# A GNN layer stack on one core: a small answer of SyncE to GpSimd behind every gather instead of behind every pair of gathers

## Chip, cores and metric

The kernel runs on one core of one Trainium2 chip. The metric is the device time of one execution in microseconds (us); the median of the runs is taken. One further execution is recorded by the hardware profiler, and all views of the profile come from that one.

## What is computed

Three layers of a relational graph network over 6250 nodes of 256 features and 100,000 edges, which come sorted by their target `dst`; then the input is added and a layer norm taken.

```python
ew = edge_attr @ edge_w + edge_b                       # 100000 x 256, from 32 attributes
for l in range(3):
    residual = x
    msg = relu(x[src] * ew)                            # x[src]: a gather of rows
    out = 0
    for i in range(3):                                 # three kinds of edge
        h = segment_sum(msg * rel_masks[i], dst) * inv_cnt[i]
        out = out + h @ weights[l, i]
    x = residual + relu(out + x @ roots[l] + biases[l])
return layernorm(x0 + x)
```

## The kernel before

**Tiles.** 128 edges make a tile, two tiles a pair (`u`, 391 of them in a layer), two pairs share one buffer `xs` of 128 x 2 x 2 x 256 floats, and there are eight such buffers (`ROWS = 8`, line 843). For each tile GpSimd (POOL in the profile) issues one indirect DMA that fetches 128 rows of 1 KB by the node numbers in `src_io`: 2346 gathers in all. In layer 0 they read the input, later `x_mid`, which the layer before has stored.

**What is done with a pair.** TensorE (PE) makes the edge weights in `ew_p` from the attributes `at` (lines 602 and 606); VectorE (DVE) multiplies them into `xs` (line 627), ScalarE (ACT) applies relu (629), VectorE makes one-hot columns of the targets (`oh`, line 635), TensorE reduces the messages into `h_p` (645), and VectorE adds that to a ring of sums `acc` (660). When a block of 128 nodes is complete, TensorE multiplies its sums by the weights (688), VectorE finishes the block (719, 722), and SyncE (SP) stores it to `x_mid` (724), or in the last layer to the output (741).

**Order.** The order of all instructions is written out by hand: one loop over steps `it` emits, for each step, the gathers of the pair nine steps ahead (`AHEAD = 9`) first, then SyncE's loads (`at`, line 560, once for eight pairs; in the last layer the input's blocks, line 748), then the work of the other engines. Each engine has its own instruction queue and goes through it in this order. The first six pairs of a layer are gathered early: for layer 0 before the main loop, into `x_root`, without the small exchange that is told of next; for the later layers at the end of the layer before (`gather_early`). Their missing rows are added by line 620 and 622. The first other gather of a layer waits until all blocks of `x_mid` have been stored, and the last block's store waits until the early gathers, which read the same tensor, have landed.

**The exchange with SyncE.** Behind the two gathers of a pair, `gather_pair` (line 899) lets GpSimd set one integer `echo` to nought (`memset`, line 905) and lets SyncE load it (line 906). Nobody uses the loaded value, and the compiled program has no load there any more: what is left on SyncE is a bare instruction that waits for the memset and counts up a semaphore (EVENT_SEMAPHORE of line 906). The next memset writes the same integer, so that GpSimd's sequencer must wait for that count first: an EVENT_SEMAPHORE of line 905 ahead of each memset. In GpSimd's instruction queue the order is: gather, gather, wait for SyncE's answer to the memset before, memset, gather, gather, wait, memset. A gather that uses an `xs` buffer again has an instruction of its own ahead of it that waits for the buffer's readers (EVENT_SEMAPHORE of line 901).

Of the kernel before, what the change touches and what calls it, by code (L numbers as in the profile page):

```python
# [442 lines left out]
def ordered_path(ctx, tc, x, attr_laid, A, weights, roots, biases, edge_w, edge_b, out, src, src_i, seg, place_i, consts, x_root,  # L443
# [126 lines left out]
    def layer(l, r_sb, b_sb, ats, early, pools):  # L570
# [12 lines left out]
        def gather(u):  # L583
            p = order.index(u)
            if p < FIRST:
                xs[u // 2] = early[u // 2]
            else:
                if first_of(p, 2):
                    xs[u // 2] = room(rows, D)
                gather_pair(nc, xs[u // 2], x_rows, src_i, u, echo)  # L590
# [18 lines left out]
        def gather_early(p):  # L609
            u = order[p]  # L610
            if first_of(p, 2):
                early_next[u // 2] = room(rows, D)
            gather_pair(nc, early_next[u // 2], x_mid[l], src_i, u, echo)
# [285 lines left out]
def gather_pair(nc, xs, x_rows, src_i, u, echo=None):  # L899
    for i in range(2):  # L900
        nc.gpsimd.indirect_dma_start(  # L901
            out=xs[:, u % 2, i, :], out_offset=None, in_=x_rows[:, :],
            in_offset=bass.IndirectOffsetOnAxis(ap=src_i[:, 2 * u + i:2 * u + i + 1], axis=0))
    if echo is not None:
        nc.gpsimd.memset(echo, 0)  # L905
        nc.values_load_multi_w_load_instructions(echo, engines=[mybir.EngineType.SP], min_val=0, max_val=0,  # L906
                                                 skip_runtime_bounds_check_because="it is nought")


@with_exitstack  # L910
def kernel(ctx, tc, x, src, dst, edge_attr, edge_type, weights, roots, biases, edge_w,
# [32 lines left out]
    with tc.tile_pool(name="look", bufs=1) as look, tc.tile_pool(name="look_p", bufs=2, space=PSUM) as look_p, \  # L944
# [17 lines left out]
        for u in schedule(N, E, 1)[0][:FIRST]:  # L962
            if u // 2 not in first_rows:
                j = 4 * len(first_rows)
                first_rows[u // 2] = x_root[:, j:j + 4, :].rearrange("p (k i) d -> p k i d", k=2)
            gather_pair(nc, first_rows[u // 2], x, src_i, u)
# [103 lines left out]
```

## Time and profile before

| | us |
|---|---|
| median of 3 runs | 2987.92 (2986.93 to 2989.48) |
| the profiled execution | 2990.14 |
| its span, from the first instruction to the last | 2988.3 |
| GpSimd busy | 2345.8 |
| TensorE: matmuls, weight loads | 2466.2, 2064.4 |
| VectorE busy | 2082.1 |
| ScalarE busy | 934.5 |

The granted TensorE clock is 0.897 on the mean. Busy time of GpSimd is that of the engine itself; what its sequencer does (waits for semaphores, hands instructions over) appears in the profile as POOLq, what SyncE's does as SPq. [...]

### The profile page before, as it was taken

The numbers are of one execution on the slowest core, as the hardware profiler recorded it, in microseconds if no ns is written. First come the engines' busy times: TensorE is split into PE (matmuls) and PEld (weight loads), VectorE is DVE, ScalarE is ACT, GpSimd is POOL, SyncE is SP. The second block draws the span as 40 slices with busy tenths as digits, with TensorE's granted clock in tenths as the row PEclk, the third lists the DMA queues.
The fourth block names the chain that finished last, engine by engine and source line by source line (L and its number), as shares of the span: only waits on it lengthen the run. The fifth ranks groups of instructions, "written<-read, shape, count | busy, mean of one in ns | idle before, by whom it ended". The sixth has DMA issues, their size and how long they took to land.

```text
span 2988.3 us, 58435 instructions
## 1 busy us (share of the span) xinstructions
PE 2466.2 (83%) x18875; PEld 2064.4 (69%) x18875; DVE 2082.1 (70%) x5868; ACT 934.5 (31%) x1155; POOL 2345.8 (78%) x3522
## 2 busy tenths in 40 slices
PE   5888888898988778888888888787888888888876
PEld 4777777777776666677676776565667677777765
DVE  7767777777776666666666666565767777787764
ACT  3333344444443222222222222222222222332221
POOL 7777787777777777777777777777777777777775
PEclk9899999999998888988999999788988989999987
DMA  5444444444444444444444444434444444444442
GB/s 169 137 144 135 145 126 127 128 128 130 132 130 118 121 130 120 125 125 123 127 128 130 127 130 133 122 120 143 133 134 139 134 131 137 137 128 129 132 124 87
DMA packets 173350, 388.09 MB, mean 130 GB/s; under 512 B 43418, under 2 KB 78636, under 8 KB 173036
## 3 DMA queue, kind: packets, MB, share of 16 engines
q0 software_dynamic: 112608, 307.65, 34.8%
q1 hardware_dynamic: 53136, 68.50, 7.4%
q10 hardware_dynamic: 7292, 8.11, 0.9%
q8 instruction: 154, 2.52, 0.3%
q14 instruction: 160, 1.31, 0.1%
HBM read 364.62 MB, written 19.46 MB: 129 GB/s over the span
## 4 chain that ended last, share of the span: by engine, by line
POOL 45%; PE 25%; issue 13%; DMA 9%; DVE 4%; ACT 1%; POOLq 1%; SPq 0%; DVEq 0%; ACTq 0%
POOL xs L901 43%; PE h_p L645 11%; DMA at<-in_attr_laid_dram 7%; PE ew_p L606 6%; PE o_p L688 5%; POOL echo L905 2%; PE r_p L673 2%; DVE xs L627 1%; DMA xs<-in_x_dram,src_io 1%; DMA xs<-x_mid,src_io 1%; ACT xs L629 1%; DVE oh L635 1%; PE ew_p L602 1%; DVE acc L660 1%; DVE x_root L719 0%
## 5 line engine op out<-in xcount | busy, mean ns | idle before, releaser
L901 POOL DMA_INDIRECT xs<-x_mid,src_io x1564 | 1490.2, 953 | 412.8 <-issue 236.7
L645 PE MATMUL h_p<-oh,xs 128*128 128x120 f32 x9336 | 1342.2, 296 | 151.6 <-DVE acc L660 87.8
L645 PEld LDWEIGHTS h_p<-oh,xs 128*128 128x128 f32 x9336 | 1252.8, 207 | 290.5 <-issue 123.2
L629 ACT ACTIVATE xs<-xs 128x1024 f32<-128x1024 f32 (+1 forms) x588 | 617.7, 1050 | 1769.3 <-DVE xs L627 1747.2
L627 DVE TENSOR_TENSOR xs<-ew_p,xs 128x512 f32<-128x512 f32 x1167 | 765.7, 684 | 555.1 <-PE ew_p L606 264.5
L901 POOL DMA_INDIRECT xs<-in_x_dram,src_io x770 | 734.2, 953 | 199.0 <-issue 117.7
L660 DVE TENSOR_TENSOR acc<-h_p,acc 128x240 f32 (+1 forms) x1173 | 518.6, 442 | 141.3 <-PE h_p L645 74.4
L606 PE MATMUL ew_p<-ew_sb,at 32*128 32x256 f32 x4692 | 401.1, 461 | 259.3 <-DMA at<-in_attr_laid_dram 255.9
L606 PEld LDWEIGHTS ew_p<-ew_sb,at 32*128 32x128 f32 x4692 | 263.9, 219 | 391.7 <-DMA at<-in_attr_laid_dram 354.9
L635 DVE TENSOR_SCALAR oh<-iota_w,seg_o 128x120 f32<-128x120 f32 x2346 | 517.7, 299 | 0.0
L688 PE MATMUL o_p<-w_sb,acc 128*128 128x256 f32 (+1 forms) x1716 | 456.8, 404 | 19.9 <-DVE acc L660 14.0
L688 PEld LDWEIGHTS o_p<-w_sb,acc 128*128 128x128 f32 (+1 forms) x1716 | 322.3, 200 | 87.8 <-issue 21.6
L719 DVE SCALAR_TENSOR_TENSOR x_root<-o_p,inv,x_root 128x256 f32<-128x256 f32 (+1 forms) x429 | 206.1, 480 | 56.4 <-PE o_p L688 49.1
L602 PE MATMUL ew_p<-bias,full_ones 3*128 3x512 bf16 x1173 | 166.9, 397 | 63.4 <-DVE xs L627 48.4
L673 PE MATMUL r_p<-r_sb,t_s 128*128 128x256 f32 x588 | 181.3, 437 | 5.9 <-ACT t_s L669 5.3
L639 ACT ACTIVATE oh_b<-oh 128x480 bf16<-128x480 f32 x196 | 117.8, 601 | 178.9 <-DVE oh L635 175.5
L705 ACT ACTIVATE acc<-zero_o 128x768 f32<-128x768 f32 (+1 forms) x150 | 140.6, 937 | 60.9 <-PE o_p L688 25.7
L673 PEld LDWEIGHTS r_p<-r_sb,t_s 128*128 128x128 f32 x588 | 117.9, 223 | 24.9 <-ACT t_s L669 9.4
L905 POOL MEMSET echo<- 1x1 int32 x1167 | 113.0, 97 | 1.2 <-SPq L906 0.9
L645 PE MATMUL h_p<-oh_b,full_ones 128*128 128x120 bf16 x782 | 108.2, 221 | 0.0
L676 DVE TENSOR_TENSOR x_root<-r_p,b_sb 128x256 f32<-128x256 f32 x147 | 61.8, 420 | 50.2 <-PE r_p L673 49.0
L645 PEld LDWEIGHTS <-full_ones 128*128 128x128 bf16 x782 | 82.7, 106 | 2.9
(93 smaller groups left out, 536.4 us busy)
## 6 DMA issues: line engine op xcount, KB each, us to landing
at<-in_attr_laid_dram SPq DMA_DIRECT2D x147, 256.0 KB
xs<-x_mid,src_io POOLq DMA_INDIRECT x1564
xs<-in_x_dram,src_io POOLq DMA_INDIRECT x770
x_mid<-x_all SPq DMA_DIRECT2D x96, 128.0 KB
x_all<-in_x_dram ACTq DMA_DIRECT2D x8, 768.0 KB
x<-in_x_dram SPq DMA_DIRECT2D x48, 128.0 KB
out_dram<-x_all SPq DMA_DIRECT2D x48, 128.0 KB
w_sb<-in_L_gnn_weights_dram SPq DMA_DIRECT2D x3, 768.0 KB
```

The source lines that it names most:

```text
L602: nc.tensor.matmul(banks[j].rearrange("p i d -> p (i d)"), full_ones[j * A:j * A + PARTS, :], bias[j * A:j * A + PARTS].rearrange("p i d - ...
L606: nc.tensor.matmul(banks[j][:, i, :], ats[OCT * o // GROUP][j * A:(j + 1) * A, o % (GROUP // OCT), i, :], ew_sb[j * A:(j + 1) * A, :], sta ...
L627: nc.vector.tensor_mul(xs[q][:, k], ew_ps[2 * q + k], xs[q][:, k])
L629: nc.scalar.activation(there, there, AF.Relu)
L635: nc.vector.tensor_scalar(ohs[q][:, t, :], iota_w, seg[:, 4 * q + t:4 * q + t + 1], None, op0=ALU.is_equal)
L645: nc.tensor.matmul(h_ps[u][:, d, :], xs[u // 2][:, u % 2, i, d * P:(d + 1) * P] if d < DC else full_ones, (ohs if d < DC else oh_bs)[u // ...
L660: nc.vector.tensor_tensor(there, h_ps[u][:, :CH].rearrange("p c (r w) -> p c r w", r=R), there, op=ALU.add)
L673: nc.tensor.matmul(rs[c][:, 1, :], t_ss[c][:, d, :], r_sb[:, d, :], start=(d == 0), stop=(d == DC - 1))
L688: nc.tensor.matmul(o_p[:n, j, :], acc[:, d, r, slot:slot + n], w_sb[:, r * DC + d, :], start=(d == 0), stop=(d == DC - 1))
L719: nc.vector.scalar_tensor_tensor(root, o_p[:n, j, :], inv[:n, c, r:r + 1], root, op0=ALU.mult, op1=ALU.add)
L901: nc.gpsimd.indirect_dma_start(out=xs[:, u % 2, i, :], out_offset=None, in_=x_rows[:, :], in_offset=bass.IndirectOffsetOnAxis(ap=src_i[:, ...
L905: nc.gpsimd.memset(echo, 0)
```

## The change

The memset and SyncE's answer move into the loop over the two gathers of a pair, so that they stand behind each gather.

```diff
     for i in range(2):
         nc.gpsimd.indirect_dma_start(
             out=xs[:, u % 2, i, :], out_offset=None, in_=x_rows[:, :],
             in_offset=bass.IndirectOffsetOnAxis(ap=src_i[:, 2 * u + i:2 * u + i + 1], axis=0))
-    if echo is not None:
-        nc.gpsimd.memset(echo, 0)
-        nc.values_load_multi_w_load_instructions(echo, engines=[mybir.EngineType.SP], min_val=0, max_val=0,
-                                                 skip_runtime_bounds_check_because="it is nought")
+        if echo is not None:
+            nc.gpsimd.memset(echo, 0)
+            nc.values_load_multi_w_load_instructions(echo, engines=[mybir.EngineType.SP], min_val=0, max_val=0,
+                                                     skip_runtime_bounds_check_because="it is nought")
```

In the compiled program that is 1167 more memsets on GpSimd with 1167 more waits for SyncE's answer ahead of them, and 1167 more answers on SyncE. The order of all other instructions is the same on every engine. GpSimd's queue becomes: gather, wait for SyncE's answer to the memset before, memset, gather, wait, memset.

## The prediction

> **What bounds the kernel.** I read the page first (busy times, the chain, the groups), then the stages, then GpSimd's own order of time.
>
> ```profile
> span 2988.3 us, 58435 instructions
> PE 2466.2 (83%) x18875; PEld 2064.4 (69%) x18875; DVE 2082.1 (70%) x5868; ACT 934.5 (31%) x1155; POOL 2345.8 (78%) x3522
> ...
> POOL 45%; PE 25%; issue 13%; DMA 9%; DVE 4%; ACT 1%; POOLq 1%; SPq 0%; DVEq 0%; ACTq 0%
> POOL xs L901 43%; PE h_p L645 11%; DMA at<-in_attr_laid_dram 7%; PE ew_p L606 6%; PE o_p L688 5%; POOL echo L905 2%; PE r_p L673 2%; DVE xs L627 1%; DMA xs<-in_x_dram,src_io 1%; DMA xs<-x_mid,src_io 1%; ACT xs L629 1%; DVE oh L635 1%; PE ew_p L602 1%; DVE acc L660 1%; DVE x_root L719 0%
> ...
> L901 POOL DMA_INDIRECT xs<-x_mid,src_io x1564 | 1490.2, 953 | 412.8 <-issue 236.7 <-SPq L906 141.1 <-PE h_p L645 8.2
> ...
> L905 POOL MEMSET echo<- 1x1 int32 x1167 | 113.0, 97 | 1.2 <-SPq L906 0.9
> ```
>
> TensorE is busiest by share, but the chain that ended last lies on GpSimd's gathers. GpSimd is 78% busy, so the question is whether its other 22% is free. The views of GpSimd's waits, of the gathers in one stage, and of its order of time say that it isn't:
>
> ```profile
> POOL xs L901 <- issue: 354.4, 1163, 0.6
> POOL xs L901 <- SPq L906: 206.8, 954, 0.2
> 1010.00:1975.00 965.00, 731.06 (x769) 0.89 0.42 126
> 62.70 0.95 POOL L901 DMA_INDIRECT xs<-in_x_dram,src_io  x1 [0.21 <-SPq L906]
> 63.95 0.95 POOL L901 DMA_INDIRECT xs<-in_x_dram,src_io  x1 [0.30 <-issue]
> 64.90 0.09 POOL L905 MEMSET echo<- 1x1 int32 x1
> 65.20 0.95 POOL L901 DMA_INDIRECT xs<-in_x_dram,src_io  x1 [0.22 <-SPq L906]
> ```
>
> In layer 1, 965 us hold 769 gathers, 965/769 = 1.255 us each, and a gather is busy 731.06/769 = 0.951. Gathers follow each other with a pause of 354.4/1163 = 0.305 that no event of the profile ends ("issue"). So GpSimd paces the kernel: a pair costs 2.51 us, whatever the rest does. An effect must change 1.25 us per gather, or GpSimd's few real stops. One nanosecond on each of 2346 gathers is 2.3 us; what a measurement of this kernel can tell from no change is about 0.2%, 6 us.
>
> **The memsets: 1167 more, put at 0.**
>
> ```profile
> L905 POOL MEMSET echo<- x1167: 88/88/255, 23.1 to 2965.3; 1x1 int32 x195
> L906 SPq EVENT_SEMAPHORE  x1168: 17/17/28, 26.6 to 2965.4; - x195
> SPq L906 <- POOL echo L905: 2744.2, 1166, 4.5
> ```
>
> A memset takes 0.088 at the median, and the pause behind it is 206.8/954 = 0.217. Together that is 0.305, the pause between two gathers without a memset. The order of time shows the same: 62.70 to 63.95 without, 63.95 to 65.20 with a memset, 1.25 each. The memset starts where the gather ends and lies inside a pause that is there anyway. Although the profile names SyncE's answer as what ended the 0.217, it can't be: gathers without it start at the same distance. So the 1167 memsets in the other pauses cost 0. If that cover failed they would cost 1167 x 0.097 (the group's mean, 113.0/1167) = 113 us, the upper bound; a gain is excluded, since no pause gets shorter with a memset in it.
>
> **The waits: the lead of GpSimd's sequencer.** Now the sequencer stops for SyncE's answer ahead of each memset, so behind a waiting instruction stands the memset and then the next gather. How early are gathers handed over today?
>
> ```profile
> L901 POOL DMA_INDIRECT xs<-in_x_dram,src_io x30: 942/946/1174, 20.7 to 58.9; - x30
> L901 POOL DMA_INDIRECT x_root<-in_x_dram,src_io x12: 942/948/1441, 5.1 to 19.4; - x12
> L901 POOLq EVENT_SEMAPHORE  x587: 17/43/43, 60.1 to 2958.0; - x196
> ```
>
> Up to 60.1 us, 30 + 12 = 42 gathers have started. The sequencer's first event of line 901, at 60.1, belongs to the first gather that uses an `xs` buffer again: after 12 gathers into `x_root` and 8 x 4 into the eight buffers, number 45, which starts at 62.70. So the sequencer works two gathers ahead, stopped by the answer. After the change it is one gather, 1.25 us, ahead. Is that enough? Two places show a gather handed over to an idle engine:
>
> ```profile
> 23.41 1.10 POOL L901 DMA_INDIRECT xs<-in_x_dram,src_io  x1 [0.15 <-issue]
> 24.82 1.10 POOL L901 DMA_INDIRECT xs<-in_x_dram,src_io  x1 [0.30 <-issue]
> 26.82 0.09 POOL L905 MEMSET echo<- 1x1 int32 x1 [0.91 <-SPq L906]
> 27.51 0.94 POOL L901 DMA_INDIRECT xs<-in_x_dram,src_io  x1 [0.59 <-issue]
> ...
> 1004.47 0.95 POOL L901 DMA_INDIRECT xs<-x_mid,src_io  x1 [0.30 <-issue]
> ...
> 1009.97 0.94 POOL L901 DMA_INDIRECT xs<-x_mid,src_io  x1 [4.47 <-DMA x_mid<-x_all]
> L901 POOLq EVENT_SEMAPHORE  x1: 43/43/43, 1009.2 to 1009.2; - x1
> L905 POOLq EVENT_SEMAPHORE  x1: 17/17/17, 1010.2 to 1010.2; - x1
> ```
>
> At 1009.2 the sequencer is released; the gather starts at 1009.97, 0.7 later, and at 1010.2 the sequencer has already handed over a second gather and stands at the next wait: 1.0 for two gathers, 0.5 each, the second while the first runs. At 26.82 the memset goes, and the gather behind it starts 0.69 later. After the change, the answer lets the sequencer go just after a memset; the gather that it then hands over is due 1.25 + 0.22 = 1.47 after that memset's end. It takes under 0.1 for the answer, 0.1 for the memset, 0.7 for the gather: 0.9. Some 0.5 us are left, so this too costs 0. The bounds: nothing, or, if no lead were left, 0.70 - 0.30 = 0.4 per gather. I take the first.
>
> **SyncE's queue.** 1167 x 17 ns = 20 us of answers, on an engine that waits 2744.2 us for these very memsets. Its DMA issues stay where they are, behind the answer to the pair's second memset, but the next answer is now due 1.25 us later instead of 2.5.
>
> ```profile
> 990.59 0.38 SPq L553 DMA_DIRECT2D r_sb<-in_L_gnn_roots_dram  x1
> 991.02 0.46 SPq L555 DMA_DIRECT2D b_sb<-in_L_gnn_biases_dram  x1
> 991.58 0.41 SPq L560 DMA_DIRECT2D at<-in_attr_laid_dram  x1
> at<-in_attr_laid_dram SPq DMA_DIRECT2D x147, 256.0 KB
> x_mid<-x_all SPq DMA_DIRECT2D x96, 128.0 KB
> x<-in_x_dram SPq DMA_DIRECT2D x48, 128.0 KB
> out_dram<-x_all SPq DMA_DIRECT2D x48, 128.0 KB
> ```
>
> The longest row of issues, at a layer's start, ends at 991.58 + 0.41 = 991.99, 1.4 after its begin: 0.2 late, under the 0.5 left. One or two issues of 0.4 fit in 1.25. So 0, at most 2 x 0.2.
>
> **The start: +2.5 us.** Here the added wait is seen. SyncE gives its first answer only at 26.6 (its row above), and today the second memset waits for it at 26.82, with gathers 15 and 16 (23.41 and 24.82) already gone. After the change the memset behind gather 14 waits, and gathers 15 and 16 stand behind it. The gather that starts at 27.51 will be the 15th instead of the 17th: two gathers at 1.25 later, 2.5 us. Nothing gives it back: the later stops, such as the 4.47 at 1009.97, begin when the last early gather has landed and shift with it.
>
> **The sum.** 0 + 0 + 0 + 2.5. Against the profiled execution's 2990.14 that is 2992.6; against the median, 2.2 lower, 2987.92 + 2.5 = **2990.4 us**, 0.08%: within what is told from no change.
>
> **The rivals.**
>
> *Late gathers (slower).* The lead of half a microsecond is worked out from idle starts; while a gather runs, handing over may take longer, and where SyncE issues a DMA the answer comes up to 0.3 to 0.4 later. Then the exchange becomes a wait on GpSimd's path at the 147 + 96 + 48 + 48 = 339 issues. It decides once handing over takes over 1.2 us. If each of these issues cost 0.05, that is 17 us, 3007; if each cost a third of a microsecond, 113 us. For it: nothing in the trace shows handing-over under load but for the second gather at 1010.2. Against it: that one was in time. Chance 0.25, at about 3007.
>
> *The memset isn't hidden (slower).* +113 us, 3103. It needs a pause of 0.305 that differs between first and second gathers of a pair; the x1163 and x954 rows speak against it. 0.07.
>
> *VectorE blocks the memset (slower).*
>
> ```profile
> L635 DVE TENSOR_SCALAR oh<-iota_w,seg_o x2346: 249/277/530, 33.4 to 2970.5; 128x120 f32<-128x120 f32 x196
> ```
>
> If a memset had to wait for the whole of a one-hot operation, it would last 0.088 + 0.277 = 0.365, 0.06 beyond the pause. 2346 x 0.277 / 2988 = 22% of the memsets would meet one: 1167 x 0.22 x 0.06 = 15 us, 3005. The longest memset of the trace is 0.255, inside the pause, among 1167, so 0.05. [...]
>
> *Fewer clashes (faster).* Gathers take 0.942 at best, 0.946 at the median, 0.953 on the mean (1490.2/1564 in the group shown at the start), so 7 ns x 2346 = 16 us go to clashes with other work. A new rhythm between GpSimd and VectorE may halve this: 8 us less, 2982. It may as well add them. 0.12.
>
> **How the numbers follow.** Forecast 0.51, late gathers 0.25, memset not hidden 0.07, blocked memset 0.05, fewer clashes 0.12. Slower by over 0.2% are the second to fourth, less 0.02 for late gathers that cost under 6 us: 0.35. Faster: 0.12. Within: 0.53. The range takes in the forecast's own, 2985 to 2996 (clashes of some us either way), half of the faster case at the low end, 2981, and late gathers up to 0.06 per issue, 2990 + 20 = 3010. Outside are the 113 us, the far end of late gathers and the rest of the faster case.
>
> **What would show it.** Right: gathers still 1.25 us apart, each with a memset of 0.088 and a pause of 0.217, x2334 memsets, the first answered memset at about 26.8 with the 15th gather behind it, the last gather about 2.5 us later. Late gathers would show as pauses over 0.22 behind memsets, ended by the answer of line 906, or as events of line 905 in GpSimd's sequencer that follow the answer by more than they do now. A hidden cost of the memset would show as a higher distance of gathers everywhere. Wrong is the whole argument if the distance of gathers in layer 1 leaves 1.255 by more than 3 ns.

## The result and the profile after

| us | before | after |
|---|---|---|
| median of 20 runs each | 2987.14 (2984.67 to 2994.27) | 2992.61 (2989.79 to 2997.78) |
| the profiled execution | 2990.14 | 2990.46 |
| its span | 2988.3 | 2988.7 |

The ratio is 1.0017, with a 95% interval of 1.0010 to 1.0023: 3.0 to 6.9 us longer, 5.5 by the medians. That is a small loss, below the 0.2% that the forecast took for what can be told from no change; but the forecast's 2.5 us lies under the interval, so the loss is about twice as large as forecast.

From the page of the changed kernel: span, busy times, the chain by engine and line, the groups of gathers and memsets. After them its view of GpSimd's waits (us in total, times, longest).

```profile
span 2988.7 us, 61936 instructions
PE 2457.0 (82%) x18875; PEld 2063.2 (69%) x18875; DVE 2080.9 (70%) x5868; ACT 934.2 (31%) x1155; POOL 2454.8 (82%) x4689
...
POOL 55%; PE 19%; issue 11%; DMA 7%; DVE 4%; POOLq 1%; ACT 1%; SPq 1%; DVEq 0%; ACTq 0%
...
L901 POOL DMA_INDIRECT xs<-x_mid,src_io x1564 | 1491.0, 953 | 338.7 <-SPq L906 309.0
...
L905 POOL MEMSET echo<- 1x1 int32 x2334 | 227.8, 98 | 4.3 <-SPq L906 3.8
```
```profile
POOL xs L901 <- SPq L906: 459.1, 2123, 0.6
...
POOL echo L905 <- SPq L906: 3.8, 1, 3.8
```

GpSimd's busy time has grown by 109 us (2454.8 - 2345.8), and the span by 0.4. The pause behind a memset is 459.1/2123 = 0.216 us, as before, and the 354.4 us of pauses put down to "issue" are now memset plus this pause. A reader who goes by the list of waits alone would say that SyncE's answer has come to hold GpSimd for 252 us more; the distance of the gathers says that it doesn't. The same 965 us of layer 1 as in the prediction, begun 2.4 us later, where this layer's first answered gather now starts (view by windows: us, GpSimd's busy time in gathers and their count, TensorE's clock, DMA share, GB/s):

```profile
1012.40:1977.40 965.00, 731.09 (x768) 0.89 0.42 125
```

965/768 = 1.2565 us for each gather, with 769 before: one gather fewer, the smallest step of such a count. The median distance of two gathers is 1.251 in both traces. The start, in GpSimd's order of time in the changed kernel:

```profile
22.11 0.95 POOL L901 DMA_INDIRECT xs<-in_x_dram,src_io  x1 [0.22 <-issue]
26.87 0.09 POOL L905 MEMSET echo<- 1x1 int32 x1 [3.82 <-SPq L906]
27.55 0.94 POOL L901 DMA_INDIRECT xs<-in_x_dram,src_io  x1 [0.59 <-SPq L906]
28.50 0.09 POOL L905 MEMSET echo<- 1x1 int32 x1
28.80 0.94 POOL L901 DMA_INDIRECT xs<-in_x_dram,src_io  x1 [0.22 <-SPq L906]
29.73 0.09 POOL L905 MEMSET echo<- 1x1 int32 x1
30.05 0.95 POOL L901 DMA_INDIRECT xs<-in_x_dram,src_io  x1 [0.23 <-SPq L906]
```

The gather at 27.55 is the 15th, so the 17th starts at 30.05, where it was 27.51 before: 2.5 us. The end, in the order of time of VectorE and GpSimd, first before, then after:

```profile
2964.37 0.94 POOL L901 DMA_INDIRECT xs<-x_mid,src_io  x1 [0.30 <-issue]
2969.34 0.69 DVE L627 TENSOR_TENSOR xs<-ew_p,xs 128x512 f32<-128x512 f32 x1 [3.48 <-DMA xs<-x_mid,src_io]
```
```profile
2968.47 0.95 POOL L901 DMA_INDIRECT xs<-x_mid,src_io  x1
2971.87 0.69 DVE L627 TENSOR_TENSOR xs<-ew_p,xs 128x512 f32<-128x512 f32 x1 [1.65 <-DMA xs<-x_mid,src_io]
```

The last gather starts 4.10 us later, but what follows it was shorter in this execution: 2988.7 - 2969.41 = 19.3 us from the last gather's end to the span's, and 23.0 before. The last rows landed earlier after it, and TensorE's clock was higher there (0.77 and 0.65):

```profile
2965.31:2988.30 22.99, 11.26 (x44) 9.49 (x43) 6.60 (x19) 2.40 (x4) 0.09 (x2) 0.65 0.06 17
```
```profile
2969.41:2988.70 19.29, 8.03 (x46) 7.02 (x45) 6.69 (x19) 2.40 (x4) 0.09 (x2) 0.77 0.07 21
```

In the profiled executions of these two kernels and of the experiments on chips like theirs this tail is between 18.4 and 23.8 us, with no order by kernel. So two spans must not be compared to the microsecond. The start of the last gather is free of the tail, but it still holds the lengths of all gathers, and in the experiments below with memsets of one integer, or with none, on chips like these two kernels' these add up to 0.25 to 1.94 us more than before. Its parts have to be told apart.

Where its 4.10 us come from I worked out from the starts and ends of all 2346 gathers in both traces. The first gather starts 0.14 later. The stop at the start is 2.90 longer (4.19 beyond the usual pause of 0.305, and 1.29 before). The two stops between layers are 0.15 shorter, the gathers themselves 0.39 shorter, the rest 0.07 shorter. What is left is new: 30 pauses of over 0.305 + 0.01 us, 1.66 us together beyond 0.305, where before had none. One of the two largest lies between 2324.99 and 2325.53 in the changed kernel:

```profile
2324.04 0.95 POOL L901 DMA_INDIRECT xs<-x_mid,src_io  x1 [0.22 <-SPq L906]
2324.99 0.09 POOL L905 MEMSET echo<- 1x1 int32 x1
2325.53 0.94 POOL L901 DMA_INDIRECT xs<-x_mid,src_io  x1 [0.46 <-SPq L906]
```

All 30 come behind a gather whose number leaves 7 when divided by 21 (112, 196, 238, 280, 364 and so on, the last 2338). There are 112 such places; 30 of them show a pause, of 0.02 to 0.24 us. Most of the 30 have something else in common: in 24 the gather that comes late uses an `xs` buffer again, so that the instruction of line 901 that waits for the buffer stands ahead of it in GpSimd's queue. Of the 111 places behind a memset 29 have that instruction, and 24 of these show a pause; of the other 82 only 6 do.

### The profile page after: what moved, and what is told of

Same layout as the page of the kernel before. It is cut to its first block, busy times and chain, and to the rows that moved or that the text cites. A ratio compares the mean times of both kernels' runs of the same rounds, so it can differ in the third digit from the quotient of the medians.

```text
span 2988.7 us, 61936 instructions
## 1 busy us (share of the span) xinstructions
PE 2457.0 (82%) x18875; PEld 2063.2 (69%) x18875; DVE 2080.9 (70%) x5868; ACT 934.2 (31%) x1155; POOL 2454.8 (82%) x4689
## 3 DMA queue, kind: packets, MB, share of 16 engines
q0 software_dynamic: 112608, 307.65, 34.9%
## 4 chain that ended last, share of the span: by engine, by line
POOL 55%; PE 19%; issue 11%; DMA 7%; DVE 4%; POOLq 1%; ACT 1%; SPq 1%; DVEq 0%; ACTq 0%
POOL xs L901 49%; PE h_p L645 8%; POOL echo L905 6%; DMA at<-in_attr_laid_dram 5%; PE o_p L688 4%; PE ew_p L606 4%; PE r_p L673 2%; DMA xs<-in_x_dram,src_io 2%; DVE xs L627 1%; SPq L906 1%; POOLq L905 1%; DMA xs<-x_mid,src_io 1%; ACT xs L629 1%; DVE oh L635 1%; DVE x_root L719 1%
## 5 line engine op out<-in xcount | busy, mean ns | idle before, releaser
L606 PE MATMUL ew_p<-ew_sb,at 32*128 32x256 f32 x4692 | 395.0, 455 | 249.8 <-DMA at<-in_attr_laid_dram 246.3
L905 POOL MEMSET echo<- 1x1 int32 x2334 | 227.8, 98 | 4.3 <-SPq L906 3.8
```

What stands on the lines that cost most here:

```text
L606: nc.tensor.matmul(banks[j][:, i, :], ats[OCT * o // GROUP][j * A:(j + 1) * A, o % (GROUP // OCT), i, :], ew_sb[j * A:(j + 1) * A, :], sta ...
```

## The experiments

All are the changed kernel but for the edit shown. The three groups ran on three chips, each group beside the kernel before on its own chip.

### The start and the lead: first group

My theory was that the start costs 2.5 us and that a lead of two gathers removes the small pauses. Before took 2987.03 us on this chip (33 runs).

*The start as before, the rest as after.*

```diff
-                gather_pair(nc, xs[u // 2], x_rows, src_i, u, echo)
+                gather_pair(nc, xs[u // 2], x_rows, src_i, u, echo, l > 0 or p >= FIRST + 2)    # each
...
-        if echo is not None:
+        if echo is not None and (i == 1 or each):
```

> The changed kernel, but the first two pairs of layer 0 that have an answer get one for each pair, as before; every other gather has its own. Theory (start plus pauses): the gather behind the first late answer is the 17th again instead of the 15th, so the last gather ends 2.5 us earlier than in the changed kernel; the some 30 pauses of 0.02 to 0.25 us (together 1.7 us) stay. Time 2.5 us under the changed kernel, about 1.7 to 2.5 above the kernel before. Rival (the added memsets disturb the rhythm of GpSimd and VectorE everywhere): the time stays where the changed kernel is, about 5 above before.

Measured: 2988.59 us, ratio 1.0009 [1.0000, 1.0018]. Its trace has the start of before again (the 17th gather at 27.70), and 33 small pauses, 2.28 us together. So the small pauses don't come from the start. The time alone would not tell: its interval reaches from 0 to 5.4 us above before.

*The kernel before, with a memset and an answer behind the first gather of the first answered pair too.* Here only that one pair is answered for each gather:

```diff
-                gather_pair(nc, xs[u // 2], x_rows, src_i, u, echo)
+                gather_pair(nc, xs[u // 2], x_rows, src_i, u, echo, l == 0 and p == FIRST)    # each; False for the early gathers
...
-        if echo is not None:
+        if echo is not None and (i == 1 or each):
```

> The kernel before, but the first pair of layer 0 that has an answer gets one behind each of its two gathers. Theory: it has the changed kernel's start alone, the 15th gather at 27.5 us, the last gather 2.5 us later than before and no pauses of 0.02 to 0.25 us, so 2.5 us above before. Rival: nothing, within 1 us of before.

Measured: 2990.22, ratio 1.0011 [1.0002, 1.0020], 3.3 us (0.6 to 6.0). By the middle of that, one memset and one answer make more than half of the 5.5. GpSimd's order of time in this kernel:

```profile
21.86 0.96 POOL L901 DMA_INDIRECT xs<-in_x_dram,src_io  x1 [0.23 <-issue]
26.75 0.09 POOL L905 MEMSET echo<- 1x1 int32 x1 [3.92 <-SPq L906]
27.43 0.94 POOL L901 DMA_INDIRECT xs<-in_x_dram,src_io  x1 [0.59 <-issue]
```

The 15th gather stands behind the late answer as in the changed kernel, and there is not one small pause. Its stop at the start is 3.01 longer than before. Its last gather starts 4.66 later all the same, because a stop between layers is longer and its gathers together last 1.18 more, which shows how little one execution's last gather says without its parts.

*Two integers in turn*, so that a memset waits for the answer to the memset before the last, and the sequencer's lead is two gathers again:

```diff
-    echo = big.tile([1, 1], I32, name="echo")
+    echo = [big.tile([1, 1], I32, name=f"echo{i}") for i in range(2)]
...
-            nc.gpsimd.memset(echo, 0)
+            nc.gpsimd.memset(echo[i], 0)
```

> The changed kernel, but the two gathers of a pair use an integer of their own each, so that a memset waits for the answer to the memset two before, and the sequencer can be two gathers ahead again, with as many instructions as in the changed kernel. Theory: the small pauses (33 over 0.315 us in the changed kernel, none before but three long ones) vanish; at the start the 16th gather, not the 15th, stands behind the late answer, so 1.25 us are lost instead of 2.5. Time 1.25 above before, some 3 under the changed kernel. Rival (pauses come from the larger number of instructions itself, or of memsets): the pauses stay, only 1.25 us are won.

Measured: 2988.57, ratio 1.0005 [0.9996, 1.0014]. No small pause is left, with the same 2334 memsets and answers. The 16th gather, not the 15th, comes first behind the late answer. So the pauses come from the lead, not from memsets or answers as such. The times of these three kernels overlap in their intervals; it is the traces that separate them.

*No memset and no answer at all.*

```diff
-        if echo is not None:
-            nc.gpsimd.memset(echo, 0)
...
```

> No memset and no answer at all. Theory (memsets and answers lie in a pause that is there anyway, and only the stop at the start costs): gathers still 1.25 us apart; the stop of 1.3 us at the start goes, time 1.3 us under before, 2986. Rival (the answers hold the sequencer back from something harmful): slower than before by over 6 us, with longer gathers or new pauses.

Measured: 2986.44, ratio 0.9999 [0.9990, 1.0008]. Without a single memset the gathers keep their distance. From this kernel's order of time:

```profile
704.23 0.95 POOL L901 DMA_INDIRECT xs<-in_x_dram,src_io  x1 [0.30 <-issue]
705.49 0.95 POOL L901 DMA_INDIRECT xs<-in_x_dram,src_io  x1 [0.30 <-issue]
706.74 0.95 POOL L901 DMA_INDIRECT xs<-in_x_dram,src_io  x1 [0.30 <-issue]
```

### What the pause covers, and where the 21 comes from: second group

This group fell to a chip on which the kernel before takes 4435.66 us (11 runs) and in whose records TensorE's clock is 0.75 to 0.84. GpSimd doesn't pace most kernels there (its memsets wait 1303.6 us for answers in the kernel with one more memset and 959.1 in the one with the memset of 128x128), so the times say nothing about the changed kernel on the first chip, and I read the traces where gathers follow each other undisturbed.

*One more memset, of an integer that nobody waits for.* My first idea of the 21 was that something recurs with the number of instructions; then one more instruction for each gather would make the grid shorter. The 18 gathers that I put for it were an estimate from a count of instructions for each gather that no run shows.

```diff
-    echo = big.tile([1, 1], I32, name="echo")
+    echo = [big.tile([1, 1], I32, name=n) for n in ("echo", "spare")]
...
+            nc.gpsimd.memset(echo[1], 0)
```

> The changed kernel with one more memset, of another integer that nobody waits for, behind each answered memset. In the changed kernel the small pauses stand 21 gathers, or multiples of 21, apart. [...] The second memset still fits in the pause of 0.305 (2 x 0.088), so the time is that of the changed kernel within 3 us. Rival (the pauses come from SyncE's loads, from blocks of nodes or another rhythm of the program): they stay 21 apart. Rival on the cover (each memset costs): 2334 x 0.09 = 210 us more.

Measured: 4637.91, ratio 1.0456 [1.0431, 1.0481]. The order of time in this kernel:

```profile
207.16 0.09 POOL L905 MEMSET echo<- 1x1 int32 x1
207.19 0.09 POOL L906 MEMSET spare<- 1x1 int32 x1
207.46 0.94 POOL L901 DMA_INDIRECT xs<-in_x_dram,src_io  x1 [0.19 <-issue]
208.40 0.09 POOL L905 MEMSET echo<- 1x1 int32 x1
208.43 0.09 POOL L906 MEMSET spare<- 1x1 int32 x1
208.71 0.95 POOL L901 DMA_INDIRECT xs<-in_x_dram,src_io  x1 [0.19 <-issue]
```

Gathers are 1.25 apart with two memsets as with one. The two overlap: the second starts 0.03 behind the first, so that together they take 0.12. Of the kernel's 43 pauses between 12 and 290 ns over the usual one, 28 stand on the grid of 21. They did not move to 18: the idea of the instructions fell.

*The memset without an answer*, on this chip:

```diff
             nc.gpsimd.memset(echo, 0)
-            nc.values_load_multi_w_load_instructions(echo, ...)
```

> The changed kernel's memset behind every gather, but no answer of SyncE and so no wait. Theory: nothing stops at the start and the lead isn't limited, so 1.3 us under before (the stop of 1.3 us at the start goes), no small pauses, gathers 1.25 us apart. Rival (the memsets themselves cost, by clashes or in the pause): above before, at the changed kernel's 5 us or more.

Measured: 3766.16, ratio 0.849 [0.8468, 0.8512]. I had expected next to nothing; on this chip the answers cost 15%. More on that at the end.

*A memset of 128x128 and one of 128x512 in place of one integer.*

```diff
-    echo = big.tile([1, 1], I32, name="echo")
+    echo = big.tile([128, 128], I32, name="echo")      # in the second kernel [128, 512]
...
-            nc.values_load_multi_w_load_instructions(echo, ...)
+            nc.values_load_multi_w_load_instructions(echo[0:1, 0:1], ...)
```

> The changed kernel with an integer tile of 128 x 128 set to nought instead of 1 x 1; the answer still loads one integer. The trace has one memset of 128 x 128, 0.204 us. Theory (a memset is free as long as it leaves some 0.06 us of the pause of 0.305, so up to 0.245): cadence still 1.25 us; time at most 15 us above the changed kernel, from memsets that clash and from an answer that comes 0.12 later. Rival (a memset is never free, its cost at 1 x 1 is only too small to see): 2334 x (0.204 - 0.088) = 271 us above the changed kernel.

> The same with 128 x 512, which by the sizes of the memsets in the trace takes some 0.45 to 0.7 us (m). Theory: beyond 0.245 each gather pays the rest, 2334 x (m - 0.245): 480 to 1060 us above the changed kernel, and the pause between a memset and the next gather falls to about 0.06 us. Rival (the memset runs beside the next gather, there is no limit): no change of the time.

Measured: 4394.42, ratio 0.9911 [0.9880, 0.9941], and 3949.97, ratio 0.8901 [0.8874, 0.8928]; neither time can be held against an expectation made for the first chip. From the order of time of the second:

```profile
207.04 0.95 POOL L901 DMA_INDIRECT xs<-in_x_dram,src_io  x1 [0.16 <-SPq L906]
207.99 0.54 POOL L905 MEMSET echo<- 128x512 int32 x1
208.69 0.95 POOL L901 DMA_INDIRECT xs<-in_x_dram,src_io  x1 [0.17 <-SPq L906]
```

The pause behind a long memset is 0.16 to 0.17, not the 0.06 that I had put as its floor. So a memset of this kind is free only up to 0.305 - 0.165 = 0.14 us, and my "free up to 0.245" fell for it. In the undisturbed stretches of the 128x128 kernel gathers are 1.34 apart, 0.09 more. With 128x512 the median distance is 1.657, 0.41 more than 1.251, where 0.54 - 0.14 is 0.40 and my theory had 0.30.

The 0.165 is no floor for memsets of one integer. In the changed kernel some of them last longer than 0.14, and the gather behind them still comes in time. The longest, in GpSimd's order of time:

```profile
2848.26 0.96 POOL L901 DMA_INDIRECT xs<-x_mid,src_io  x1 [0.23 <-SPq L906]
2849.21 0.26 POOL L905 MEMSET echo<- 1x1 int32 x1
2849.52 1.11 POOL L901 DMA_INDIRECT xs<-x_mid,src_io  x1
```

It has 0.05 behind it, and the pause between the two gathers is 0.305 as ever. So how much room the pause has depends on the memset; why a large one needs 0.165 behind it and a small one that takes long does not, no run shows.

### The scratch, the answer, the length: third group

The kernel is built with `dynamic_dma_scratch_size=4096`, by its name a scratch for dynamic DMAs; the profile lists the queue of the gathers' 307.65 MB as software_dynamic. My second idea was a guess: that GpSimd goes through this scratch as a ring, and that the grid of 21 is the turn of that ring. No trace shows such a ring. Before took 2987.00 us on this chip (19 runs).

*Half the scratch, and twice of it.*

```diff
-    nc = _bacc.Bacc(..., dynamic_dma_scratch_size=4096)
+    nc = _bacc.Bacc(..., dynamic_dma_scratch_size=2048)     # in the second kernel 8192
```

> The changed kernel with dynamic_dma_scratch_size=2048 in place of 4096, nothing else. Theory of the ring (the small pauses of the changed kernel, which stand at every 21st gather, come where GpSimd's ring of DMA descriptors turns over, and a lead of one gather doesn't cover it): half the ring turns over after about half the gathers, so the pauses stand on a grid of 10 gathers, and there are about twice as many (60 for 30, 3 us for 1.7); the time is 1 to 3 us above the changed kernel. Rival (the 21 comes from the tables or the buffers of the kernel, not from the ring): the grid stays 21, with some 30 pauses, and the time is that of the changed kernel within 2 us. If TensorE's clock on this chip is so low that GpSimd doesn't pace the kernel, the grid alone is read.

> The changed kernel with dynamic_dma_scratch_size=8192 in place of 4096, nothing else. Theory of the ring: a grid of 42 gathers and about half the pauses (15, under 1 us); the time is 0 to 1 us under the changed kernel. Rival (tables or buffers): the grid stays 21, with some 30 pauses and 1.7 us.

Measured: 2990.75, ratio 1.0013 [1.0004, 1.0023] with 2048, and 3020.60, ratio 1.0108 [1.0091, 1.0125] with 8192. The rival (a grid of 21 in any case) fell, and so did the numbers of my theory: I had expected more pauses with half the scratch and fewer with twice of it. With 2048 there is none (none over 0.011). With 8192 there are 47, at every 49th gather without exception, of 0.59 to 0.72 us, together 29.7; 3020.60 - 2990.75 = 29.9. One of them, in GpSimd's order of time with 8192, and then the sequencer's two events of line 905 on either side of it (duration, then first and last start):

```profile
578.07 0.94 POOL L901 DMA_INDIRECT xs<-in_x_dram,src_io  x1 [0.22 <-SPq L906]
579.00 0.09 POOL L905 MEMSET echo<- 1x1 int32 x1
580.02 0.94 POOL L901 DMA_INDIRECT xs<-in_x_dram,src_io  x1 [0.93 <-ACT oh_b L639]
```
```profile
L905 POOLq EVENT_SEMAPHORE  x1: 17/17/17, 577.9 to 577.9; - x1
...
L905 POOLq EVENT_SEMAPHORE  x1: 17/17/17, 579.8 to 579.8; - x1
```

The memset at 579.00 ends at 579.09, and SyncE's answer follows 0.04 later; the sequencer comes to it only at 579.8. Something ahead of it in GpSimd's queue held it from 577.9 to 579.8, 1.9 us, where the distance of such events is otherwise 1.25. ScalarE, whom the profile names as what ended the wait of 0.93, has nothing to do with it: in other such places it names SyncE or TensorE. At all 47 places the two events are 1.79 to 1.91 us apart (once 2.11), with the answer there 0.04 behind the memset. So at every 49th gather the handing over of a gather takes about 1.8 to 1.9 us, more than the lead of one gather covers. Where the gather handed over uses its buffer again (13 of the 47 places), the pause is longer, 0.69 on the mean for 0.61 at the others: line 901's instruction costs some 0.08.

The three sizes go together if the longer handing over grows with the scratch: 0.6 us beyond the lead with 8192, just at its edge with 4096 (30 of 112 places show it, by a mean of 0.055), inside it with 2048. That 4096 is at the edge fits the 24 of 30 pauses at which line 901's instruction is added; that there is a longer handing over with 2048 at all is not seen. The changed kernel with 4096 was not run on this chip, but the last kernel below has 4096: in 11 places its gather comes later behind the memset than the usual 0.165, and all 11 are on the grid of 21 (112, 196, 280 and so on). So the chip is not what took the grid away. That the scratch sets the grid and the length is shown by the edit of that one number; what the sequencer does at that place is not in the trace and stays open. With a lead of two gathers the place stays hidden with 4096 (two integers in turn, and before). The kernel before with 8192 was not run.

*The memset without an answer, on a chip like the first.*

> Each gather is followed by a float set to zero, as in the changed kernel, but SyncE answers none and GpSimd waits for none: 2334 memsets without an answer. All theories that hold the memset free: gathers 1.25 us apart as in both kernels, no small pauses, no stop at the start; where GpSimd paces the kernel, 1 to 2 us under the kernel before and 5 to 7 us under the changed one. If the memset cost what lies beyond a free pause, say 0.02 us for each, it would be 40 us above the kernel before.

Measured: 2985.90, ratio 0.9994 [0.9985, 1.0004]. Its 2334 memsets cost nothing that can be measured; the count by windows (us, gathers' busy time and count, clock, DMA share, GB/s) is that of before, 749 gathers in 940 us, 1.255 each:

```profile
1030.00:1970.00 940.00, 712.08 (x749) 0.92 0.43 126
```

*The memset of 128x128, on a chip like the first.*

> The changed kernel with a memset of 128x128 floats in place of one float. By the trace of this kernel on the other chip (0.226 us for the memset, 0.165 to 0.17 behind it, gathers 1.34 apart): 0.09 us for each of 2334 gathers, 210 us above the changed kernel, so about 3200 us, where GpSimd paces the kernel. By my older bound (a memset is free up to 0.245 us): no more than 5 us above the changed kernel.

Measured: 3197.85, ratio 1.0730 [1.0683, 1.0776]; about 207 above the changed kernel with 2048, which ran beside it, for 210 expected. Its groups by line (the memset's busy time and mean) and its order of time:

```profile
L905 POOL MEMSET echo<- 128x128 int32 x2334 | 528.7, 227 | 4.9 <-SPq L906 3.8
```
```profile
1500.17 0.95 POOL L901 DMA_INDIRECT xs<-x_mid,src_io  x1 [0.17 <-SPq L906]
1501.12 0.22 POOL L905 MEMSET echo<- 128x128 int32 x1
1501.50 0.95 POOL L901 DMA_INDIRECT xs<-x_mid,src_io  x1 [0.17 <-SPq L906]
```

0.22 + 0.165 is 0.08 beyond the pause, for each of 2334 gathers; over all gathers the pauses beyond 0.305 come to 196 us, and the gathers themselves are 8 us longer than with 2048. Each nanosecond that every memset adds to GpSimd's path counts 2334 times here, 1167 times for the memsets that the change adds: 5 ns for each would have been 6 us.

## Why the forecast held, step by step

**GpSimd paces the kernel: right.** 0.08 us on every gather (the 128x128 memset) made the kernel 7% slower; 0.63 at every 49th, 1%.

**The memsets at 0: right, by the reason given.** The pause stayed at 0.305 with no, one and two memsets. The prediction left open how much room there was: for the large memsets it is 0.14 us, and of the memsets of one integer, 0.088 at the median, even the longest, 0.263, cost nothing.

**VectorE blocks the memset: memsets are longer beside its one-hot operations, at no price.** 308 of the changed kernel's 2334 memsets last over 0.11 us, and all 308 run beside a TENSOR_SCALAR of VectorE, 298 of them beside the one-hot operations of line 635; none that runs beside VectorE's other operations alone, or beside none, is that long. 250 others run beside a TENSOR_SCALAR and last no longer than 0.11; what makes the difference no run shows. But the longest is 0.263, not the 0.365 that the rival needed, and it still lies inside the pause, as shown above:

```profile
L905 POOL MEMSET echo<- x2334: 88/88/263, 21.8 to 2969.4; 1x1 int32 x195
```

**The sequencer's lead at 0: mis-sized, by 1.7 us.** The step read: handing a gather over takes 0.7, the lead is one gather, some 0.5 us are left. That holds for the ordinary gather. But the 0.5 was read from two ordinary places, and handing over isn't the same for all: on a grid of 21 gathers it takes so long that little or nothing is left, and 30 times the gather comes late, 1.66 us in all, 24 of these times where the sequencer has the buffer's waiting instruction to go through as well. The rival "late gathers" had the right mechanism (a lead that no longer covers handing over) in the wrong place: not at SyncE's 339 DMA issues, which show no pause of their own, but on a grid that the DMA scratch sets, and at a tenth of its price. With a scratch of 8192 the same step costs 30 us, and the changed kernel takes 3020.60, outside the range of 2981 to 3010. That the term is small with 4096 is luck: nothing in the prediction looked at it.

**SyncE's queue at 0: right on chips like the first**, by the same grid: no small pause of the changed kernel stands off it.

**The start, +2.5: right.** 2.54 at the 17th gather, 3.3 [0.6, 6.0] in time for that edit alone. The stop itself is 2.90 longer; some of that comes back before the 17th gather, as gathers 14 to 16, of 1.10 to 1.17 each in the kernel before, now take 0.94 to 0.95.

**The sum.** 2.5 was forecast, under the measured 3.0 to 6.9. The two causes shown, the stop at the start with 2.90 and the small pauses with 1.66, make 4.6, and 4.1 is what the starts of the last gather show in one execution each; both lie inside that interval. Of the rest to the 5.5 of the medians, about 1 us, no run says whether it is there. Fewer clashes with other work, the faster rival, are not shown: the gathers are 0.39 us shorter in this execution, less than such executions differ (1.94 us at most, as said above).

## What to carry to other kernels

When an engine that issues gathers sets the pace, look for the pause between two of them and for how far its sequencer runs ahead: here work inside the pause was free up to a length that had to be measured for that kind of work (0.14 us for the large memsets), and then cost its full excess on every gather (0.08 us, about 207 in all, with 128x128), and the wait on another engine's answer was free only where the lead covered the slowest handing over, not the median one (a lead of 1.25 us covered the 0.7 of an ordinary gather, not the 1.8 to 1.9 of every 49th with a scratch of 8192, which cost 30 us). The slowest may recur so seldom that two quoted places don't show it; compute the gaps between all of them, number them, and look whether the numbers of the long ones have a common step. A list of waits that names a new releaser is no evidence of a cost: the distance of the paced instructions is. Here the list had 252 us more for the answer, and the median distance was 1.251 in both traces.

## What the runs showed of the hardware that was not expected

**More DMA scratch made the kernel slower.** 2048: no pause; 4096: a grid of 21 gathers, 0.055 us on the mean at the 30 of 112 places that show one; 8192: every 49th, 0.63; all with a lead of one gather. 2990.75 us with 2048 and 3020.60 with 8192 on one chip, 2992.61 with 4096 on another.

**The same answer is free on one chip and costs 15% on another.** On the chip of the second group GpSimd's waits and SyncE's (us in total, times, longest) in the kernel with the 128x128 memset were:

```profile
POOL echo L905 <- SPq L906: 959.1, 144, 14.5
```
```profile
SPq L724 <- DVE x_all L722: 676.1, 75, 16.5
```

By these waits, SyncE's store of a finished block waits for VectorE, the answers stand behind the store in SyncE's queue, and GpSimd waits for the answer. Without answers the same chip took 3766.16 us for 4435.66; the cost is shown by that edit, its path is read from the waits. TensorE's clock is lower there, 0.758 for 0.897 in the kernel before on the first chip, and ahead of its matmuls of line 645 TensorE stands idle for 730.8 us that no event of the profile ends, for 51.9. Why it stands idle so long there, and why the kernel with the 128x512 memset, whose GpSimd hardly waits for answers (3.5 us), was faster than before on that chip, is open; the changed kernel itself was not run there.
